# Routed rows turned in 32-blocks by VectorE instead of by TensorE, and loaded in quarters

## The chip, the cores and the metric

The kernel runs on one core of one Trainium2 chip. The core has TensorE (PE, matrix products), VectorE (DVE), ScalarE (ACT), GpSimd (POOL) and SyncE (SP); SP issues most of the loads and stores, POOL issues the indirect ones, and 16 DMA engines carry them. The metric is the device time of one execution in microseconds (us). The kernel before takes 1947.31 us, the median of three runs (1946.74 to 1948.36).

## What is computed

The program is a model of two layers on T = 2048 rows of D = 512 float32 features. Layer 0 is a recurrence over time with a feed-forward part of two experts. Layer 1 is an attention over 16 heads whose older keys are averaged in blocks of 64, and a mixture of experts. Only the second mixture is touched by the change. Cut to what matters it is:

```python
x = x + attn0(norm(x)) * silu(ffn0(norm(x)))      # layer 0
flat = layernorm(x)                               # layer 1: 2048 x 512
h = relu(flat @ shared_w1 + shared_b1)            # two shared experts, 512 -> 352 -> 512
out = flat + h @ shared_w2 + shared_b2            # summed over the two
scores = sigmoid(flat @ centroids.T) + bias       # 16 routed experts
gating = top_4(scores) / sum(top_4(scores))
for w1, b1, w2, b2, g in routed_experts:
    out += (relu(flat @ w1 + b1) @ w2 + b2) * g[:, None]
x = x + attn1(flat) * silu(out)
```

The kernel does not run all 16 experts on all rows: each row goes to its four experts only.

## The kernel before, in words

P = 128 rows make a tile, and NC = 4 chunks of 128 features make a row. The kernel is written in a tile framework. A scheduler at compile time gives each engine a list of instructions from the order of the source, the dependences, and the buffers that each pool has; on the chip each engine runs its list in order and waits on semaphores. A pool's `bufs` says how many tiles of one name may be alive.

**Router stage** (lines 848 to 881, near 990 to 1060 us). In blocks of rows, `xr` is loaded, the first layer's result is added (L854) and statistics are taken (`norm_stats`, L122). L861 writes the normalized row tile into `acc[:, i, 0:D]`, a large array that keeps 544 values (DX) per row: 512 features, 16 gates, the row's number and a flag. `transposed` (L135 to L140) then has PE transpose its four chunks through the PSUM pool `m1y` (two buffers, shared with `pl`), and ACT copies them into `xT`, where features lie on the partitions. After every four tiles, PE forms the 16 expert scores (`pl`, L870). When all are known, the slots are computed, and 64 indirect DMAs of POOL (L1043, names kept in `sent`) write each row of `acc` four times to the DRAM array `xs`, sorted by expert, in tiles of 128 rows. Three further stages lie between: the shared experts (`hidden_shared`, `down_shared`), the fold of attention's weights, and again shared experts. In `down_shared` L1111 adds the normalized rows from `acc` to the result and stores it in `comb`, which starts the sum.

**Routed stage** (lines 1657 to 1741, from 1340 us). The loop over j has 80 tile slots (NRT). Tiles 0 to 64 run always; a slot after them stands in a `tc.If` block, which the count of tiles decides on the chip, and 9 of them ran here, 74 tiles in all. An `If` block is scheduled as a unit of its own: no engine's instruction crosses its edges. One step of the loop does this:

- `hidden_rows(j)`: SP reads the tile's expert number into a register. It issues one DMA for the rows, `x` (L1671, 272 KB, four buffers), which must come after all of `sent`, and four for the weights (`load1`, L654: w1 of 704 KB at L659, w2 of 512 KB at L660, w3 of 192 KB at L661, b2 at L662; three buffers each). The first three tiles load weights ahead of rows, the others after. PE transposes the four chunks (L1678) into `tp`, one PSUM bank of the pool `m1t`. ACT copies `tp` to `xg` (L1680, three buffers). PE forms 12 products (`ph`, L1685: the 352 hidden features in three parts, times 4 chunks; the profile has two instructions for each), and ACT applies bias and relu (`ht`, L942). DVE picks the gate of the tile's expert (`junk`, `g`, L1693) and the row number to write to (`to`, L1698 and L1703).
- a piece of attention for the next tiles (`attend`), which shares PE, DVE, ACT and the PSUM pool `aps` (three banks).
- `down_rows(j - 1)`: three products on PE (`py`, L1709, again two instructions each), the gate multiplied by DVE (`y`, L1714), and two indirect DMAs of POOL that add the two halves of the row to `comb` in DRAM (L1717).

**Last rows** (L1752 to L1769). `comb` is loaded again (L1758), goes through silu on ACT, is multiplied with attention's result (L1765), added to the layer's input (L1768) and stored.

Of the kernel before, what the change touches and what calls it, by code (L numbers as in the profile page):

```python
# [9 lines left out]
F32 = mybir.dt.float32  # L10
I32 = mybir.dt.int32
AF = mybir.ActivationFunctionType
ALU = mybir.AluOpType
AX = mybir.AxisListType
PSUM = bass.MemoryType.PSUM
AFTER = mybir.DependencyInfo(mybir.DependencyClass.Sync, mybir.DependencyReason.DATA)

P = 128
# [49 lines left out]
NF1 = len(FCH)  # L68
NRT = T * KR // P + NR
DX = D + 32  # L70


def bc(ap, axis, shape):
# [4 lines left out]
def tile_kernel(ctx: ExitStack, tc: tile.TileContext, a: dict):  # L78
# [56 lines left out]
    def transposed(pool, src, dst, tag):  # L135

        tp = pool.tile([P, NC, P], F32, tag=tag, name="tp")
        for c in range(NC):
            nc.tensor.transpose(tp[:, c, :], src[:, c * P : (c + 1) * P], ident)
        nc.scalar.copy(dst, tp)  # L140
# [707 lines left out]
    for b in range(NRB):  # L848
# [9 lines left out]
        mv, rstd = norm_stats(xr, n)  # L858
        for s in range(n):
            i = i0 + s  # L860
            nc.vector.tensor_scalar(  # L861
                out=acc[:, i, 0:D], in0=xr[:, s, :], scalar1=mv[:, s, 0:1],
                scalar2=rstd[:, s : s + 1], op0=ALU.subtract, op1=ALU.mult,
            )
            transposed(m1y, acc[:, i, :], xT[:, :, i * P : (i + 1) * P], "py")
        if (i + 1) % (TB // P) == 0:
            t0 = i + 1 - TB // P
            pl = m1y.tile([NR, TB], F32, tag="py", name="pl")
# [230 lines left out]
    def down_shared(tb, hT):  # L1099
        for s in range(TB // P):  # L1100
            t = tb * (TB // P) + s
            py = m1y.tile([P, D], F32, tag="py", name="py")
            for e, w in enumerate(ws):
                for f, n in enumerate(rows_of):
                    nc.tensor.matmul(  # L1105
                        out=py, lhsT=hT[0:n, e, f, s * P : (s + 1) * P],
                        rhs=down(w, f, n), start=(e == 0 and f == 0),
                        stop=(e == NS - 1 and f == NF1 - 1),
                    )
            y = m1s.tile([P, D], F32, tag="y", bufs=3, name="y")  # L1110
            nc.vector.tensor_tensor(out=y, in0=py, in1=acc[:, t, 0:D], op=ALU.add)  # L1111
            for h, c_ in enumerate(comb):
                nc.sync.dma_start(
                    out=c_[t * P : (t + 1) * P, :], in_=y[:, h * D // 2 : (h + 1) * D // 2]
                )
# [200 lines left out]
    logps.close()  # L1316


    aps = ctx.enter_context(tc.tile_pool(name="aps", bufs=3, space=PSUM))
    QB = 256  # L1320

    def softmax(s, heads, keys, neg, wt=None, last=True):
# [206 lines left out]
    sh.close()  # L1529


    m1t = ctx.enter_context(tc.tile_pool(name="m1t", bufs=1, space=PSUM))
    aq = ctx.enter_context(tc.tile_pool(name="aq", bufs=1))
    aq2 = ctx.enter_context(tc.tile_pool(name="aq2", bufs=2))
    fin = ctx.enter_context(tc.tile_pool(name="fin", bufs=NT))
# [121 lines left out]
    def hidden_rows(j):  # L1657
# [9 lines left out]

        if j < FIRST:
            w = weights()
        x = m1x.tile([P, DX], F32, tag="x", bufs=4, name="x")  # L1670
        got = nc.sync.dma_start(out=x, in_=xs[j * P : (j + 1) * P, :])  # L1671
        for name in sent:
            tc.add_manual_dep(got.ins, name, AFTER, reason="any of them may hold its rows")
        if j >= FIRST:
            w = weights()
        tp = m1t.tile([P, NC, P], F32, tag="tp", name="tp")
        for c in range(NC):
            nc.tensor.transpose(tp[:, c, :], x[:, c * P : (c + 1) * P], ident)  # L1678
        xg = m1x.tile([P, NC, P], F32, tag="xg", name="xg")
        nc.scalar.copy(xg, tp)  # L1680
        hT = hts[j % len(hts)]
        for f, n in enumerate(FCH):
            ph = m1ps.tile([P, P], F32, tag="ph", name="ph")
# [7 lines left out]
        junk = m1x.tile([P, NR], F32, tag="junk", name="junk")  # L1691
        g = m1x.tile([P, 1], F32, tag="g", name="g")
        nc.vector.tensor_tensor_reduce(  # L1693
            out=junk, in0=x[:, D : D + NR], in1=oh[:, j, :], scale=1.0, scalar=0.0,
            op0=ALU.mult, op1=ALU.add, accum_out=g,
        )

        nc.vector.scalar_tensor_tensor(  # L1698
            out=junk[:, 0:1], in0=x[:, D + NR + 1 : D + NR + 2], scalar=away[:, 1:2],
            in1=x[:, D + NR : D + NR + 1], op0=ALU.mult, op1=ALU.add,  # L1700
        )
        to = m1x.tile([P, 1], I32, tag="to", bufs=6, name="to")
        nc.vector.tensor_tensor(out=to, in0=junk[:, 0:1], in1=away[:, 0:1], op=ALU.add)  # L1703
# [159 lines left out]
```

## Time and profile before

| What | us | From |
|---|---|---|
| median of three runs | 1947.31 | the times |
| the profiled execution | 1949.3 | the times |
| span of the profiled execution | 1947.6, clock 0.98 | the profile |
| PE, DVE, ACT, POOL busy | 1846.0, 784.7, 527.8, 466.1 | the profile |
| transposes of routed rows (L1678) | 296 instructions, 273 ns each | groups by form |
| copy of the transposed rows (L1680) | 74 instructions, 586 ns each | groups |
| normalizing (L861) | 16 instructions, 548 ns each | groups by form |
| y add of the shared experts (L1111) | 16 instructions, 688 ns each | groups by form |
| DMA over the span | 381.36 MB, 196 GB/s on average | the profile |

Here is how to read a profile of this kind. It is one execution on the chip. A row of a group gives the line, the engine, the operation, output and inputs by name with their shapes, the count, then busy time and the mean of one instruction, then the idle time of the engine just ahead of them and what ended it. PE's matmuls are pipelined, so the mean of one can be longer than the distance to the next. PEld is the load of the stationary operand, which overlaps PE. SPq is SP's issue of a DMA. A table by stage gives busy time and the number of instructions of each engine in a stretch of the span, the granted clock of PE as a share of full speed, and the mean busy share of the 16 DMA engines. The chain of waits follows the work that ended last back to what released it; its rows here are in order of time.

### The profile page before, as it was taken

What the parts mean: (1) busy time and instruction counts of PE and PEld (TensorE: products, weight loads), DVE (VectorE), ACT (ScalarE), POOL (GpSimd) and SP (SyncE); (2) the same over time, 40 slices, a digit from 0 to 9 for tenths busy, and PEclk for the clock granted to TensorE, in tenths of its full rate; (3) what the DMA queues carried; (4) which work ended last, traced back from release to release, by engine and by line L of the source; (5) the groups of instructions that cost most, each with busy time, mean ns of one, the idle gap of its engine ahead of it and who ended that gap; (6) DMA issues with size and microseconds to landing.
All of it is one profiled execution on the core that took longest, in us unless ns stands there. A gap on an engine that the chain in (4) does not pass through costs nothing.

```text
span 1947.6 us, 23278 instructions
## 1 busy us (share of the span) xinstructions
PE 1846.0 (95%) x8107; PEld 1287.3 (66%) x8107; DVE 784.7 (40%) x1581; ACT 527.8 (27%) x997; POOL 466.1 (24%) x350
## 2 busy tenths in 40 slices
PE   5899999999999999999989999999999999999990
PEld 4677777777877777777534744445777777777660
DVE  8713536272725444341276444321332333232213
ACT  6213232232423232321234122221222222222222
POOL 1301112120212010110300561000434443333341
PEclk9899999999999999999999999999999999999995
DMA  7557785625563443437451652025999999888896
GB/s 252 204 172 246 243 288 194 215 94 177 164 224 106 152 141 118 131 126 276 130 182 55 219 191 84 31 81 173 289 311 325 270 279 265 247 250 245 223 273 189
DMA packets 214609, 381.36 MB, mean 196 GB/s; under 512 B 17484, under 2 KB 134988, under 8 KB 213592
## 3 DMA queue, kind: packets, MB, share of 16 engines
q1 hardware_dynamic: 184408, 332.78, 51.3%
q0 software_dynamic: 28784, 45.63, 10.6%
q10 hardware_dynamic: 1296, 1.41, 0.2%
q8 instruction: 67, 1.10, 0.2%
q14 instruction: 54, 0.44, 0.1%
HBM read 294.04 MB, written 85.72 MB: 195 GB/s over the span
## 4 chain that ended last, share of the span: by engine, by line
PE 84%; DMA 6%; DVE 3%; issue 2%; POOL 2%; ACT 2%; SPq 1%; DVEq 0%; POOLq 0%; ACTq 0%
PE pg L571 23%; PE py L593 12%; PE ph L1685 9%; PE py L1709 9%; PE proj L416 7%; PE py L1105 4%; PE ph L956 3%; DMA comb<-y,to 3%; PE pq L1352 2%; PE pw L1593 2%; PE tp L1678 1%; PE ps L1560 1%; PE po L712 1%; PE ps L1566 1%; PE pl L870 1%
## 5 line engine op out<-in xcount | busy, mean ns | idle before, releaser
L571 PE MATMUL pg<-xg,w 128*128 128x256 f32 (+1 forms) x2304 | 495.0, 367 | 3.7 <-ACT xg L563 3.7
L571 PEld LDWEIGHTS pg<-xg,w 128*128 128x128 f32 x2304 | 419.0, 190 | 94.6 <-issue 42.1
L1717 POOL DMA_INDIRECT comb<-y,to x146 | 227.4, 1557 | 343.0 <-DMA comb<-y,to 140.5
L593 PE MATMUL py<-wd,hT 128*128 128x512 f32 x544 | 256.9, 593 | 2.8 <-DVE hT L578 2.8
L1685 PEld LDWEIGHTS ph<-xg,w 128*128 128x128 f32 (+1 forms) x1776 | 202.3, 182 | 37.6 <-ACT xg L1680 31.4
L1685 PE MATMUL ph<-xg,w 128*128 128x128 f32 (+1 forms) x1776 | 213.9, 277 | 1.6 <-DMA w<-in_w_dram 1.6
L1709 PE MATMUL py<-w,ht 128*128 128x512 f32 (+1 forms) x438 | 207.6, 593 | 0.0
L578 DVE TENSOR_TENSOR hT<-sg,pg 128x256 f32<-128x256 f32 (+1 forms) x144 | 56.9, 400 | 335.8 <-ACT sg L576 335.7
L576 ACT ACTIVATE sg<-pg 128x256 f32<-128x256 f32 (+1 forms) x144 | 53.5, 372 | 416.8 <-PE pg L571 416.5
L1714 DVE TENSOR_SCALAR y<-py,g 128x512 f32<-128x512 f32 x73 | 54.6, 748 | 247.6 <-PE py L1709 247.4
L593 PEld LDWEIGHTS py<-wd,hT 128*128 128x128 f32 x544 | 102.1, 190 | 72.1 <-issue 62.0
L942 ACT ACTIVATE ht<-ph,b1t 128x128 f32<-128x128 f32 (+1 forms) x222 | 81.3, 366 | 178.6 <-PE ph L1685 154.2
L1709 PEld LDWEIGHTS py<-w,ht 128*128 128x128 f32 (+1 forms) x438 | 76.7, 191 | 56.2 <-issue 54.0
L1680 ACT COPY xg<-tp 128x512 f32<-128x512 f32 x74 | 43.3, 586 | 179.9 <-PE tp L1678 176.5
L1105 PE MATMUL py<-w,hT 128*128 128x512 f32 (+1 forms) x192 | 89.3, 596 | 0.0
L956 PE MATMUL ph<-xT,w 128*128 128x512 f32 (+1 forms) x192 | 88.0, 597 | 0.0
L1043 POOL DMA_INDIRECT xs<-acc,slot x64 | 63.0, 985 | 67.1 <-DMA xs<-acc,slot 42.8
L712 PE MATMUL po<-wo,yb 128*128 128x512 f32 x128 | 58.4, 612 | 7.6 <-ACT acc L721 3.7
L416 PE MATMUL proj<-xm,wr 128*128 128x256 f32 x256 | 60.5, 391 | 4.3 <-ACT v L452 4.3
L464 POOL TENSOR_TENSOR ex<-st_p,qt 128x1024 f32<-128x1024 f32 x8 | 18.3, 2288 | 193.0 <-DVE qt L463 193.0
L1678 PEld LDWEIGHTS tp<-ident,x 128*128 128x128 f32 x296 | 36.7, 140 | 38.8 <-issue 20.8
L545 POOL DMA_INDIRECT xr<-in_x_dram,tok x17 | 23.2, 1367 | 160.3 <-PE tp L560 133.2
(417 smaller groups left out, 2198.3 us busy)
## 6 DMA issues: line engine op xcount, KB each, us to landing
w<-in_w_dram SPq DMA_DIRECT2D x76, 704.0 KB
w<-in_w_dram SPq DMA_DIRECT2D x76, 512.0 KB
w<-in_w_gate_dram SPq DMA_DIRECT2D x72, 512.0 KB
w<-in_w_up_dram SPq DMA_DIRECT2D x72, 512.0 KB
wd<-in_w_down_dram SPq DMA_DIRECT2D x72, 512.0 KB
xs<-zero SPq DMA_DIRECT2D x16, 1360.0 KB
x<-xs SPq DMA_DIRECT2D x74, 272.0 KB
w<-in_w_dram SPq DMA_DIRECT2D x76, 192.0 KB
```

Source lines behind the costliest of these rows:

```text
L416: nc.tensor.matmul(out=ps[:, j, :], lhsT=w_[:, c, (o0 + j) * P : (o0 + j + 1) * P], rhs=xm[:, c, :], start=(c == 0), stop=(c == NC - 1),)
L571: nc.tensor.matmul(out=pg[:, i, 0:n], lhsT=w[:, c, i * FH + f * P : i * FH + (f + 1) * P], rhs=xg[:, c, 0:n], start=(c == 0), stop=(c == N ...
L578: nc.vector.tensor_tensor(out=hT[:, 0:n], in0=sg[:, 0:n], in1=pg[:, 1, 0:n], op=ALU.mult)
L593: nc.tensor.matmul(out=p, lhsT=hT[:, u * P : (u + 1) * P], rhs=wd[:, f, :], start=first_, stop=last_,)
L712: nc.tensor.matmul(out=po, lhsT=yb[:, c, s * P : (s + 1) * P], rhs=wo[:, c, :], start=(c == 0), stop=(c == NC - 1),)
L942: nc.scalar.activation(dst, src, AF.Relu, bias=b)
L956: nc.tensor.matmul(out=ph[0:n, :], lhsT=up(w, f, n, c), rhs=xT[:, c, cols], start=(c == 0), stop=(c == NC - 1),)
L1043: ins = nc.gpsimd.indirect_dma_start(out=xs, out_offset=bass.IndirectOffsetOnAxis(ap=slot[:, i, k : k + 1], axis=0), in_=acc[:, i, :], in_ ...
L1105: nc.tensor.matmul(out=py, lhsT=hT[0:n, e, f, s * P : (s + 1) * P], rhs=down(w, f, n), start=(e == 0 and f == 0), stop=(e == NS - 1 and f ...
L1685: nc.tensor.matmul(out=ph[0:n, :], lhsT=up(w, f, n, c), rhs=xg[:, c, :], start=(c == 0), stop=(c == NC - 1),)
L1709: nc.tensor.matmul(out=py, lhsT=hT[0:n, f, :], rhs=down(w, f, n), start=(f == 0), stop=(f == NF1 - 1),)
L1717: nc.gpsimd.indirect_dma_start(out=c_, out_offset=bass.IndirectOffsetOnAxis(ap=to, axis=0), in_=y[:, h * D // 2 : (h + 1) * D // 2], in_of ...
```

## The change

It consists of these parts.

- The rows lie in `acc` and `xs` with their 32-feature blocks in another order: feature block q of chunk c, formerly at place 4c + q, lies at place 4q + c. L861 therefore writes the normalized row to a new tile `xn` (two buffers). PE transposes from `xn`, and a new ACT copy puts `xn` into `acc` with its blocks reordered. L1111 reads `acc` with a matching access pattern.
- The load of a routed tile is split: for each q of 4, one DMA takes 128 columns of the tile's 128 rows (64 KB) and puts them onto 32 partitions, so that partition 32q + r holds row r of each 32-row block. A fifth DMA loads the last 32 columns into `own`, with a row to a partition. All five depend on `sent`.
- One DVE instruction, `nc.vector.transpose`, turns the 32x32 blocks of `x` and writes `xg`. PE's four transposes and ACT's copy are gone.
- `junk` and `to` take their inputs from `own` instead of from `x`.
- The PSUM pool `m1t` goes, and `aps` gets a fourth bank.

```diff
--- before.py
+++ after.py
@@ -68,6 +68,8 @@
 NF1 = len(FCH)
 NRT = T * KR // P + NR
 DX = D + 32
+NB = 4
+BL = P // NB
 
 
 def bc(ap, axis, shape):
@@ -858,11 +860,17 @@
         mv, rstd = norm_stats(xr, n)
         for s in range(n):
             i = i0 + s
+            xn = tr.tile([P, D], F32, tag="xn", bufs=2, name="xn")
             nc.vector.tensor_scalar(
-                out=acc[:, i, 0:D], in0=xr[:, s, :], scalar1=mv[:, s, 0:1],
+                out=xn, in0=xr[:, s, :], scalar1=mv[:, s, 0:1],
                 scalar2=rstd[:, s : s + 1], op0=ALU.subtract, op1=ALU.mult,
             )
-            transposed(m1y, acc[:, i, :], xT[:, :, i * P : (i + 1) * P], "py")
+            transposed(m1y, xn, xT[:, :, i * P : (i + 1) * P], "py")
+
+            nc.scalar.copy(
+                acc[:, i, 0:D].rearrange("p (q c k) -> p q c k", q=NB, k=BL),
+                xn.rearrange("p (c q k) -> p q c k", q=NB, k=BL),
+            )
         if (i + 1) % (TB // P) == 0:
             t0 = i + 1 - TB // P
             pl = m1y.tile([NR, TB], F32, tag="py", name="pl")
@@ -1108,7 +1116,11 @@
                         stop=(e == NS - 1 and f == NF1 - 1),
                     )
             y = m1s.tile([P, D], F32, tag="y", bufs=3, name="y")
-            nc.vector.tensor_tensor(out=y, in0=py, in1=acc[:, t, 0:D], op=ALU.add)
+            nc.vector.tensor_tensor(
+                out=y.rearrange("p (c q k) -> p c q k", q=NB, k=BL),
+                in0=py.rearrange("p (c q k) -> p c q k", q=NB, k=BL),
+                in1=acc[:, t, 0:D].rearrange("p (q c k) -> p c q k", q=NB, k=BL), op=ALU.add,
+            )
             for h, c_ in enumerate(comb):
                 nc.sync.dma_start(
                     out=c_[t * P : (t + 1) * P, :], in_=y[:, h * D // 2 : (h + 1) * D // 2]
@@ -1316,7 +1328,7 @@
     logps.close()
 
 
-    aps = ctx.enter_context(tc.tile_pool(name="aps", bufs=3, space=PSUM))
+    aps = ctx.enter_context(tc.tile_pool(name="aps", bufs=4, space=PSUM))
     QB = 256
 
     def softmax(s, heads, keys, neg, wt=None, last=True):
@@ -1529,7 +1541,6 @@
     sh.close()
 
 
-    m1t = ctx.enter_context(tc.tile_pool(name="m1t", bufs=1, space=PSUM))
     aq = ctx.enter_context(tc.tile_pool(name="aq", bufs=1))
     aq2 = ctx.enter_context(tc.tile_pool(name="aq2", bufs=2))
     fin = ctx.enter_context(tc.tile_pool(name="fin", bufs=NT))
@@ -1667,17 +1678,25 @@
 
         if j < FIRST:
             w = weights()
-        x = m1x.tile([P, DX], F32, tag="x", bufs=4, name="x")
-        got = nc.sync.dma_start(out=x, in_=xs[j * P : (j + 1) * P, :])
-        for name in sent:
-            tc.add_manual_dep(got.ins, name, AFTER, reason="any of them may hold its rows")
+
+        x = m1x.tile([P, NB, NC, BL], F32, tag="x", bufs=4, name="x")
+        own = m1x.tile([P, DX - D], F32, tag="own", bufs=4, name="own")
+        mine = xs[j * P : (j + 1) * P, :]
+        loads = [
+            nc.sync.dma_start(
+                out=x[q * BL : (q + 1) * BL].rearrange("p b c k -> p b (c k)"),
+                in_=mine[:, q * P : (q + 1) * P].rearrange("(b r) k -> r b k", r=BL),
+            )
+            for q in range(NB)
+        ]
+        loads.append(nc.sync.dma_start(out=own, in_=mine[:, D:]))
+        for got in loads:
+            for name in sent:
+                tc.add_manual_dep(got.ins, name, AFTER, reason="any of them may hold its rows")
         if j >= FIRST:
             w = weights()
-        tp = m1t.tile([P, NC, P], F32, tag="tp", name="tp")
-        for c in range(NC):
-            nc.tensor.transpose(tp[:, c, :], x[:, c * P : (c + 1) * P], ident)
         xg = m1x.tile([P, NC, P], F32, tag="xg", name="xg")
-        nc.scalar.copy(xg, tp)
+        nc.vector.transpose(xg.rearrange("p c (b r) -> p b c r", r=BL), x)
         hT = hts[j % len(hts)]
         for f, n in enumerate(FCH):
             ph = m1ps.tile([P, P], F32, tag="ph", name="ph")
@@ -1691,13 +1710,13 @@
         junk = m1x.tile([P, NR], F32, tag="junk", name="junk")
         g = m1x.tile([P, 1], F32, tag="g", name="g")
         nc.vector.tensor_tensor_reduce(
-            out=junk, in0=x[:, D : D + NR], in1=oh[:, j, :], scale=1.0, scalar=0.0,
+            out=junk, in0=own[:, 0:NR], in1=oh[:, j, :], scale=1.0, scalar=0.0,
             op0=ALU.mult, op1=ALU.add, accum_out=g,
         )
 
         nc.vector.scalar_tensor_tensor(
-            out=junk[:, 0:1], in0=x[:, D + NR + 1 : D + NR + 2], scalar=away[:, 1:2],
-            in1=x[:, D + NR : D + NR + 1], op0=ALU.mult, op1=ALU.add,
+            out=junk[:, 0:1], in0=own[:, NR + 1 : NR + 2], scalar=away[:, 1:2],
+            in1=own[:, NR : NR + 1], op0=ALU.mult, op1=ALU.add,
         )
         to = m1x.tile([P, 1], I32, tag="to", bufs=6, name="to")
         nc.vector.tensor_tensor(out=to, in0=junk[:, 0:1], in1=away[:, 0:1], op=ALU.add)
```

## The prediction

> **What bounds the kernel.** I read the page first, then a table of busy time by stage, then the groups of instructions by form, the timeline of the last tiles, and the waits.
>
> ```profile
> PE 1846.0 (95%) x8107; PEld 1287.3 (66%) x8107; DVE 784.7 (40%) x1581; ACT 527.8 (27%) x997; POOL 466.1 (24%) x350
> ```
>
> TensorE is busy for 95% of the span. The change acts in the router stage (1013 to 1060 us) and in the routed stage (from 1340 on), so those rows decide. Columns: us, then busy time and count of PE, PEld, DVE, ACT, POOL, then clock, DMA share, GB/s.
>
> ```profile
> 1013.00:1043.00 30.00, 25.42 (x114) 10.77 (x112) 14.77 (x32) 12.96 (x25) 0.00 (x0) 1.00 0.05 18
> 1043.00:1060.00 17.00, 17.00 (x44) 7.49 (x45) 13.67 (x54) 7.37 (x13) 2.06 (x8) 1.00 0.35 110
> 1340.00:1348.00 8.00, 6.23 (x34) 4.69 (x32) 3.11 (x16) 1.76 (x3) 0.39 (x2) 1.00 0.90 304
> 1348.00:1839.00 491.00, 490.81 (x2708) 355.16 (x2708) 145.19 (x462) 125.83 (x296) 193.24 (x124) 1.00 0.94 272
> 1839.00:1898.00 59.00, 57.10 (x335) 40.44 (x334) 11.81 (x46) 16.36 (x40) 24.85 (x16) 1.00 0.95 280
> 1898.00:1948.00 50.00, 0.00 (x0) 0.00 (x0) 19.35 (x32) 11.14 (x17) 9.31 (x6) 0.50 0.64 185
> ```
>
> From 1348 to 1839 us PE is busy for 490.8 of 491 us at full clock, with tiles 0 to 63: 7.67 us a tile, attention pieces included. DMA runs at 0.94 beside it, so it is second, and not far off. After 1898 PE has nothing to do: the scatter-adds and the last rows finish.
>
> What the four transposes really take of PE, the timeline of one tile in the `If` blocks shows (start, us, engine, line):
>
> ```profile
> 1856.98 0.60 PE L1678 MATMUL tp<-ident,x 128*128 128x128 f32 x4
> ...
> 1857.41 1.02 PE L1709 MATMUL py<-w,ht 97*128 97x512 f32 x2
> ...
> 1858.31 2.92 PE L1685 MATMUL ph<-xg,w 128*128 128x128 f32 x24
> ```
>
> The next instruction starts 0.43 us after the first transpose, and the chain of waits lists each set as 0.44 us of path. The page's 273 ns for one of them is latency; four of those would be 1.09 us, far too much. The 24 matmuls follow xg without a hole.
>
> **The saving.** PE loses 4 transposes a tile: 0.435 us, 7.67 becomes 7.24 in the middle. The sets of tiles 0 to 2 lie in PE's wait for the first weights (1342.8 to 1348.2; the row `PE ph L1685 <- DMA w<-in_w_dram` ends it) and save nothing. Tiles 3 to 64: 62 × 0.435 = **27.0 us**. The last 9 tiles are in the tail below. ACT loses 74 copies of 586 ns, off the path.
>
> **The transpose on DVE.** No DVE transpose is in this trace. Rows near it, 128x512 f32 on DVE: 548 ns (L861), 688 (L1111), 748 (L1714). The Trainium skill ("VectorE: DVE Perf Modes", section "The three transpose paths") speaks against the move: it sends a 128×128 transpose to TensorE and gives VectorE 311 ns for one of bf16, so four would be 1.24 us, an estimate. By the row I take 0.65; ends 0.55 and 1.24. Either way 74 of them are 41 to 92 us on an engine that is busy for 145 of 491 us, so the middle stage hides it. The condition is that it runs ahead: the scheduler puts the small gate operation `junk`, which depends on the same load, as early as its three buffers let it, and xg has three buffers too. In an `If` block it can't cross the block's edge: it stands behind y of the tile before (0.75 us), and PE may wait up to 0.2 + 0.75 + 0.65 + 0.15 = 1.75 us a tile. This goes into the tail.
>
> **The loads.** One DMA of x (272 KB, 128 packets of 2176 B at 88 ns in the records = 0.70 us of 16 engines) becomes four of 64 KB and one of 16 KB. The records show 27 ns for packets of 512 B: 512 × 27 + 128 × 10 (small ones, estimated) = 15.1 us / 16 = 0.95, so +0.25 us of DMA a tile. The skill ("SBUF — State Buffer", section "Door 1: The DMA port swizzle") says that 32 neighbouring partitions reach only 8 of 16 ports, 27.2 GB/s each: 64 KB then take 0.30 us, four 1.2, about +0.6 by estimate. The trace's nearest case, sixteen loads of `vo` onto 16 partitions each, shows 84 ns for packets of 2048 B, as on 128 partitions. I take +0.25; ends 0.2 and 0.6. Against some 5.9 us of demand a tile, 6.2 to 6.5 still fit in 7.24.
>
> The queue is the worse matter. SP issues in order, 0.47 us apart:
>
> ```profile
> 1506.85 0.37 SPq L659 DMA_DIRECT2D w<-in_w_dram  x1
> 1507.32 0.37 SPq L1671 DMA_DIRECT2D x<-xs  x1
> 1507.78 0.40 SPq L1344 DMA_DIRECT2D sn<-in_sin_dram  x1
> ```
>
> Five DMAs for one are +4 × 0.47 = 1.9 us of SP a tile, hidden while SP waits:
>
> ```profile
> SPq L660 <- PE py L1709: 221.9, 57, 7.0
> ...
> SPq L660 <- DMA w<-in_w_dram: 8.5, 6, 2.4
> ```
>
> 222 us over 57 tiles is 3.9 us of slack a tile, less 0.43 for the shorter period: 1.5 stay. But SP's DMAs share eight completion semaphores: in the `vo` loads seven leave by 1290.4, the eighth only at 1294.4, when the first has landed. Each DMA waits for the eighth before it. Today a tile has 5 DMAs, so 1.6 tiles are in flight; then 9, and 0.9 of a tile: w1 of a tile can leave only after that of the tile before has landed, about 1.0 us earlier. The period is at least 1.0 + landing time of w1. That is 5.85 us in the middle (9 in 10 under 6.8): 6.85 against 7.24, so PE still decides, with 0.4 to spare. I add 1 us for tiles where it doesn't. Queued behind a waiting load on SP are the weights of its tile, cs, sn and xo; PE waits for the weights.
>
> **Start and early tiles.** Fifteen loads instead of three stand ahead of what follows, 12 × 0.47 = 5.6 us if all are in front; three of them were issued ahead of the weights of 1342.3. Part can go in the hole before. Ends 0 and 5, I take **+3**. In the first ten tiles weights arrive 1 to 2 us ahead of PE, landing in up to 9.8 us: ten savings of 0.435 are lost to them, **+4**.
>
> **Router stage.** The normalized row goes to `xn`, with two buffers, so normalizing, formerly done ahead (990 to 1013) for most rows, must wait for PE's transposes and ACT's new copy. ACT gains 16 copies; SBUF-to-SBUF copies of 512 elements take 548 to 720 ns here, I take 0.63: 10 us beside 13 of 30. DVE gains about 13 us beside 14.8 of 30. Neither fills the stage, but each pl group of four tiles (3.6 us of PE) now waits for DVE, PE, ACT in turn, two buffers deep: four groups by about 1 us, **+4**, ends 0 and 10. The block order in the y add (16 × 688 ns, in 203 us where PE is full) costs nothing; should it double, 11 us stay hidden there. The fourth bank for attention's scores can only take waits away from 1060 to 1137, where PE idles 2.75 of 77: **−1**, ends −3 and 0.
>
> **Tail.** In the last 9 tiles the path is already the scatter-adds', about 6.9 us a tile from 1854 to 1917, PE's 5.8 under it:
>
> ```profile
> 1854.47 6.34 DMA comb<-y,to
> ...
> 1861.54 5.96 DMA comb<-y,to
> ...
> 1868.33 6.07 DMA comb<-y,to
> ```
>
> The blocks reuse the same semaphores in the same order, 9 loads for 8, so b2 waits for the first x load of its own block, and the next block's first load for b2: 9 × 0.5 + 4.4 (landing of b2 there) ≈ 8.9 us a tile. SP enters two tiles ahead (15 us), so PE ends 9 × 8.9 − 15 − 59 = 6 us later relative to its start, while the backlog of scatter-adds (20 us after PE now) shrinks. **+3**, ends −8 and +12.
>
> **Sum.** −27.0 + 4 (early) + 3 (start) + 4 (router) − 1 (bank) + 3 (tail) + 1 (queue) = −13 on the profiled 1949.3 (span 1947.6 and 1.7 around it): 1936. The profiled execution is 2.0 above the median of 1947.3, so **1934 us**, −0.7%. A measurement of this kernel can tell 0.2%, 3.9 us: faster is below 1943.4, slower above 1951.2.
>
> **Rivals.**
> A, slower: the eight semaphores bound the routed stage. The weights of the next tile no longer load beside this tile's, so every tile takes 1.0 + landing time. It cancels the saving from a landing of 6.7 us on (1.0 + 6.7 = 7.67), against 5.85 now and 6.8 in the slow tenth; the five loads add traffic that lengthens it. At 6.9 the period is 7.9: 62 × 0.23 = +14, with start, router and tail +10: 1971. Against it: fewer loads in flight land sooner, and DMA has room. 0.28, mostly 1953 to 1975.
> B, nothing: the middle saves its 27, but router (+10), start (+5), early tiles (+4) and tail (+8) at their upper ends give it all back: 1947. 0.14.
> C, all of it: the losses hide in existing waits and the tail gains with PE, −27 − 2: 1918 to 1920. 0.11.
> D, it doesn't do what it says: DVE's transpose stands behind y, as in the `If` blocks, in every tile, and PE waits 1.75 for 0.435 saved: 64 × 1.3 = +84, 2030. The early `junk` speaks against it: 0.03.
> The forecast has 0.44, from 1924 to 1944.
>
> Range: leaving out D, the far part of A and half of C: 1917 to 1966. Faster 0.54 (0.43 of the forecast, C), same 0.14 (B and an edge), slower 0.32 (A, D, a rest of B).
>
> **What would show it.** The middle stage's PE time per tile should be 7.2 us with PE still full and no tp rows; a hole at `PE ph <- DMA w` or SP's waits for `DMA w` or `DMA x` growing by 60 us or more shows A; `PE ph <- DVE xg` shows D. DVE's transpose row should read 550 to 1240 ns. SP's x loads in the last blocks should come some 9 us apart. The router stage should be 31 to 40 us long instead of 30, and the first ph start 3 us later after pq. The largest doubt is w1's landing time at 9 loads a tile: half a microsecond turns the sign.

## The result, and the profile after

The changed kernel takes 1975.36 us (median of four runs, 1974.10 to 1982.43) against 1947.84 us for the kernel before on the same occasions (1946.74 to 1951.71). The ratio is 1.0133, with a 95% interval of 1.0113 to 1.0152: slower, where 1934 us and a gain of 0.7% had been forecast, and outside the range of 1917 to 1966 us. The profiled execution of the changed kernel took 1982.4 us, with a span of 1980.7 us. It is the longest of the four runs, so its sums are some 7 us above the median.

PE's share of the span fell from 95 to 92%, in the page's first part:

```profile
PE 1826.9 (92%) x7811; PEld 1268.4 (64%) x7811; DVE 818.6 (41%) x1655; ACT 493.2 (25%) x941; POOL 468.0 (24%) x350
```

The stages come next, in the table by stage (us, then busy time and count of PE, PEld, DVE, ACT, POOL, then clock, DMA share, GB/s). The rows are the router stage, the hole ahead of the first ph, tiles 0 to 63, the last tiles, and the last rows.

```profile
1018.00:1057.00 39.00, 29.96 (x113) 11.52 (x112) 28.87 (x66) 25.60 (x47) 0.00 (x0) 0.87 0.30 108
1351.00:1365.00 14.00, 12.55 (x52) 9.41 (x50) 5.68 (x13) 0.00 (x0) 1.11 (x6) 1.00 0.72 235
1365.00:1874.00 509.00, 468.24 (x2445) 333.74 (x2445) 173.92 (x532) 89.32 (x234) 196.00 (x126) 0.99 0.97 262
1874.00:1940.00 66.00, 52.36 (x294) 36.08 (x294) 16.71 (x56) 10.96 (x30) 28.80 (x19) 1.00 0.94 247
1940.00:1981.00 41.00, 0.00 (x0) 0.00 (x0) 19.36 (x32) 11.24 (x17) 2.25 (x2) 0.52 0.66 213
```

The reader is to see two things. PE did lose the work: from 490.8 to 468.2 us for the same 64 tiles. But the stage grew from 491 to 509 us, since PE now stands still in it. The view of waits (engine, line, releaser, then us in total, times, longest), for the stretch from 1340 to 1945 us, says where. These are all of PE's rows in it:

```profile
PE ph L1704 <- DVE xg L1699: 39.4, 28, 1.5
PE ps L1577 <- DVE qg L1377: 7.4, 4, 2.2
PE pw L1604 <- ACT sT L1601: 7.1, 11, 0.7
PE ph L1704 <- issue: 1.5, 1, 1.5
```

In the kernel before, PE's two rows there come to 2.0 us, and the longer of them is the first weights:

```profile
PE ph L1685 <- DMA w<-in_w_dram: 1.6, 1, 1.6
```

In the changed kernel no row names a load: neither x nor w. PE waits for VectorE's turn of its own tile; the row with `issue` is the first tile's. Of the 28 waits for xg, 9 are in the `If` blocks and 19 in tiles 1 to 64. The timeline of one tile shows the pattern (start, us, engine, line, and in brackets the idle time before it and its releaser):

```profile
1897.56 2.74 PE L1728 MATMUL py<-w,ht 128*128 128x512 f32 x6
...
1900.34 0.75 DVE L1733 TENSOR_SCALAR y<-py,g 128x512 f32<-128x512 f32 x1 [5.08 <-PE py L1728]
1901.01 0.70 DVE L1699 STREAM_TRANSPOSE xg<-x 128x512 f32<-128x512 f32 x1
...
1901.76 2.92 PE L1704 MATMUL ph<-xg,w 128*128 128x128 f32 x24 [1.46 <-DVE xg L1699]
```

VectorE's list has the turn of the next tile behind y, and y waits for py. PE's list has that tile's ph right behind py. So y (0.75 us) and the turn (0.70 us) run while PE has nothing to do, 1.46 us. In the kernel before, the last third of py stood between the transposes and ph and hid ACT's copy. PE's list changed as well. Before, ph of a tile, pieces of attention and py of an earlier tile alternate, and py stands right behind its own ph in 2 of the first 65 tiles; now it does so in all 65. Attention's pieces stand together between the tiles, where PE has the second and third row of waits.

The loads were not late. Counted from their semaphores, the five row loads of tile 70 leave SP from 1899.7 us on and have landed at 1905.7; its turn starts at 1914.9. In the middle it is the same: those of tile 30 have landed at 1588.0, its w1 at 1589.6, and its ph starts at 1603.5.

SP's own waits (from 1330 to 1950 us) did change, and would mislead if read alone. L661 is the issue of w1, L662 that of w2:

```profile
SPq L661 <- DMA w<-in_w_dram: 53.3, 49, 2.6
...
SPq L662 <- PE py L1728: 24.6, 26, 1.1
```

SP now waits for landed loads, where it waited 222 us for a weight buffer that py had to free. With the first row it runs into its eight semaphores; but as PE waits for no load, this is time that SP had to spare.

The 33 us between the two profiles, stage by stage (by the ends of the last `po`, the last `pl`, the first ph, the last product of PE and the last row):

| Stretch | before | after | difference |
|---|---|---|---|
| up to the last `po` (not touched by the change) | 1013.5 | 1018.2 | +4.8 |
| router stage, to the last `pl` | 29.5 | 38.7 | +9.2 |
| to the first ph of a routed tile | 305.2 | 308.0 | +2.8 |
| to PE's last product | 547.9 | 574.6 | +26.7 |
| to the end | 51.5 | 41.2 | −10.3 |

The fourth row is PE's busy time 547.9 to 520.7 (−27.2) and its holes 0 to 53.9.

In the router stage the chain of waits shows two of the four groups of scores in the kernel before (start, us, what):

```profile
1024.64 3.62 PE pl L870 x8
1031.97 3.62 PE pl L870 x8
```

and the second and third of them in the changed kernel, with loads of ACT's function table around the third (L133 is the square root of the statistics, L798 the sigmoid of the scores):

```profile
1029.72 5.32 PE pl L878 x8
...
1036.23 1.28 ACT L798
...
1040.25 1.28 ACT L133
...
1042.37 6.16 PE pl L878 x8
```

The eight products of a group are the same work; their granted clock was 1.00 before, and 0.68 and 0.59 in these two.

### The profile page after: what moved, and what is told of

Its sections match the earlier page's. It is cut to its first block, busy times and chain, and to the rows that moved or that the text cites. A ratio compares the mean times of both kernels' runs of the same rounds, so it can differ in the third digit from the quotient of the medians.

```text
span 1980.7 us, 23066 instructions
## 1 busy us (share of the span) xinstructions
PE 1826.9 (92%) x7811; PEld 1268.4 (64%) x7811; DVE 818.6 (41%) x1655; ACT 493.2 (25%) x941; POOL 468.0 (24%) x350
## 3 DMA queue, kind: packets, MB, share of 16 engines
q0 software_dynamic: 28784, 45.63, 10.3%
## 4 chain that ended last, share of the span: by engine, by line
PE 77%; DMA 10%; issue 3%; DVE 3%; ACT 2%; POOL 2%; SPq 1%; DVEq 0%; ACTq 0%; POOLq 0%
PE pg L573 23%; PE py L595 11%; PE ph L1704 8%; PE proj L418 7%; PE py L1728 7%; PE py L1113 4%; PE ph L964 3%; DMA w<-in_w_dram 3%; DMA comb<-y,to 3%; PE pq L1364 2%; PE pw L1604 2%; PE po L714 1%; PE ps L1571 1%; PE pl L878 1%; DVE xg L1699 1%
## 5 line engine op out<-in xcount | busy, mean ns | idle before, releaser
L1704 PEld LDWEIGHTS ph<-xg,w 128*128 128x128 f32 (+1 forms) x1776 | 207.2, 185 | 74.5 <-DVE xg L1699 62.6
L1704 PE MATMUL ph<-xg,w 128*128 128x128 f32 (+1 forms) x1776 | 216.0, 279 | 40.9 <-DVE xg L1699 39.4
L1728 PE MATMUL py<-w,ht 128*128 128x512 f32 (+1 forms) x438 | 200.2, 593 | 0.0
L578 ACT ACTIVATE sg<-pg 128x256 f32<-128x256 f32 (+1 forms) x144 | 53.4, 371 | 419.6 <-PE pg L573 419.3
L418 PEld LDWEIGHTS proj<-xm,wr 128*128 128x128 f32 x256 | 49.4, 194 | 16.5 <-ACT v L454 5.8
L418 PE MATMUL proj<-xm,wk 128*128 128x256 f32 x256 | 59.7, 388 | 0.0
```

The lines of the kernel that those rows point to most:

```text
L418: nc.tensor.matmul(out=ps[:, j, :], lhsT=w_[:, c, (o0 + j) * P : (o0 + j + 1) * P], rhs=xm[:, c, :], start=(c == 0), stop=(c == NC - 1),)
L1704: nc.tensor.matmul(out=ph[0:n, :], lhsT=up(w, f, n, c), rhs=xg[:, c, :], start=(c == 0), stop=(c == NC - 1),)
L1728: nc.tensor.matmul(out=py, lhsT=hT[0:n, f, :], rhs=down(w, f, n), start=(f == 0), stop=(f == NF1 - 1),)
```

## The experiments

Each ratio is to the kernel before on the same chip, with its 95% interval. "Holes" are PE's idle time between the first ph and its last product, from the profile of the run. "Close" is the number of the first 65 tiles whose py stands right behind its own ph in PE's list; it is 2 in the kernel before and 65 in the changed one.

**One load (e1).** The four quarter loads and `own` become the one load of the kernel before; the turn stays on VectorE.

```diff
-        loads = [nc.sync.dma_start(out=x[q * BL : (q + 1) * BL]..., in_=mine[:, q * P : (q + 1) * P]...) ...]
-        loads.append(nc.sync.dma_start(out=own, in_=mine[:, D:]))
+        got = nc.sync.dma_start(out=x, in_=xs[j * P : (j + 1) * P, :])
```

> The changed kernel with x loaded again by one DMA of 272 KB, a row to a partition; VectorE turns the 32x32 blocks of that tile, and the gate reads its last columns from it. The rows are then not where the products want them, so only the time is meant. Theory 'order' (nine loads a tile instead of five make the scheduler write py of a tile right behind its ph, and the turn of tile k+1 right behind y of tile k, so PE waits 1.46 us where no attention piece lies between): with five loads the turns stand two tiles ahead and py one tile late, the waits of ph for xg in tiles 0 to 64 fall from 28 us to under 5, the waits in attention's pieces (14 us) go too, tiles 0 to 64 take some 465 us instead of 509, the router stage keeps its 9 us: about 1937 us. Rival 'turn' (the turn on VectorE holds PE up whatever the loads are): the 1.46 us holes stay, 1965 to 1975. Rival 'semaphores' (loads land too late with nine a tile) gives 1937 as well and is not told apart here.

Measured: 1936.32 us, ratio 0.9916 (0.9890 to 0.9942). From the first ph to PE's last product 518.9 us instead of 574.6, holes 6 us, and no wait for xg among them; the waits inside attention's pieces are gone too. Close is 3. In VectorE's list the turn of a tile mostly stands behind y of the tile five before it; in the changed kernel it stands behind y of the tile just before it. So the turn itself, 701 ns on VectorE, does not hold PE; how the loads are written does, directly or through the lists. The number was expected (some 1937), but a rival, loads that land too late, gives the same.

**The five loads with PE's transposes (e2).**

```diff
-        nc.vector.transpose(xg.rearrange("p c (b r) -> p b c r", r=BL), x)
+        tp = m1t.tile([P, NC, P], F32, tag="tp", name="tp")
+        for c in range(NC):
+            nc.tensor.transpose(tp[:, c, :], x[:, c].rearrange("p c k -> p (c k)"), ident)
+        nc.scalar.copy(xg, tp)
```

> The changed kernel with its five row loads, but with the four transposes on PE and the copy on ACT as before (and three banks for attention again); the rows are not where the products want them, so only the time is meant. Theory 'order': the loads land some ten us ahead of their tile, so PE never waits for a load; the transposes of the next tile can be placed ahead of py, so no 1.46 us holes; what stays is up to 14 us of waits in attention's pieces and 9 us of the router stage: 1955 to 1968 us. Rival 'semaphores': the routed stage stays as slow as in the changed kernel or slower by the 27 us of transposes, 1975 to 2000, and SP's waits for landed loads stay near 110 us.

Measured: 1988.16 us, ratio 1.0190 (1.0172 to 1.0208). By the number alone this is the rival's. Its waits for the same stretch are not:

```profile
PE ph L1708 <- ACT xg L1703: 26.3, 36, 0.7
PE pw L1605 <- ACT sT L1602: 4.9, 11, 0.8
```

PE waits for loads for 0.7 us in all. The lists changed here too: in 36 tiles the transposes stand right ahead of ph, and ACT's copy (0.7 us) lies open. My number for the "order" theory was wrong because I took it that the transposes would stay ahead of py.

**The turn one tile ahead (e3).** The load and turn of tile j+1 are written in step j. Number, size and queue of the loads stay.

```diff
+        if j == 0:
+            turned.append(turned_rows(0))
+        if j + 1 < NRT:
+            turned.append(turned_rows(j + 1))
...
+        xg, own = turned.pop(0)
```

> The changed kernel with the five row loads and the turn of tile j+1 written in step j, ahead of the products of tile j, in the If blocks too. Everything else, the number of loads too, is as in the changed kernel. Theory 'order': the 29 holes of 1.46 us ahead of ph go, in tiles 0 to 64 (28 us) and in the If blocks (13 us, of which the scatter-adds behind give back about half); the waits in attention's pieces stay: 1938 to 1948 us. Rivals 'semaphores' and 'turn': no change, 1970 to 1978.

Measured: 1958.81 us, ratio 1.0031 (1.0019 to 1.0042), about 20 us less than the changed kernel's ratio gives on this chip, but not quite the forecast. Tiles 0 to 63 take 482.5 us instead of 509.0, and the whole stretch 548.4 instead of 574.6. This is the cleanest test. Close is 65 as in the changed kernel, and the turn stands one y further ahead. The row loads are issued a tile earlier too, but they had lain ready before. The 28 waits for xg are gone. All waits of PE over 5 us that are left:

```profile
PE ph L1713 <- DMA w<-in_w_dram: 11.7, 6, 3.2
PE ps L1577 <- DVE qg L1377: 7.2, 4, 2.2
PE pw L1604 <- ACT sT L1601: 7.1, 11, 0.7
```

The first row is new: with PE faster, the weights become the next limit, above all in the `If` blocks (w1 of tile 66 lands at 1855.1, its ph starts at 1855.3). That is a wait for loads, as rival A has it, at some 7 us a tile, behind the one that decided. Whether the eight semaphores hold the loads back or the DMA engines, which are busy throughout there (share 1.02 from 1841 to 1907 us), these rows don't tell.

**The router part alone, on the kernel before (e4).**

```diff
+            xn = tr.tile([P, D], F32, tag="xn", bufs=2, name="xn")
             nc.vector.tensor_scalar(
-                out=acc[:, i, 0:D], in0=xr[:, s, :], scalar1=mv[:, s, 0:1],
+                out=xn, in0=xr[:, s, :], scalar1=mv[:, s, 0:1],
...
+            nc.scalar.copy(acc[:, i, 0:D], xn)
```

> The kernel before with one part of the change alone: the normalized row goes to xn (two buffers), PE transposes from xn, and ACT copies it to acc in the old block order. Theory: the statistics of later rows slip behind the scores of earlier ones, ACT changes its table six times where it did once, and the router stage is 8 to 10 us longer with nothing after it to take that up: 1955 to 1958 us. Rival (the stages behind it take it up, and the 9 us seen between the profiles is their own spread): 1946 to 1950.

Measured: 1963.11 us, ratio 1.0055 (1.0034 to 1.0075): +11 us, a little over the 8 to 10 expected, with 39.5 us from the last `po` to the last `pl`, and 548.8 us with PE full in the routed stage. So the router part costs its 9 to 11 us by itself.

**The quarter loads on ACT's queue (e5).**

```diff
-            nc.sync.dma_start(
+            nc.scalar.dma_start(
                 out=x[q * BL : (q + 1) * BL].rearrange("p b c k -> p b (c k)"),
```

> The changed kernel with the four quarter loads of x issued by ACT's queue instead of SP's; own and the weights stay on SP. Nine DMAs a tile, their bytes and their packets are as in the changed kernel. Theory 'order' (in a form the first runs allow: what turns the order of PE's and VectorE's lists is how many loads stand in SP's queue a tile, and the chip's DMA is not the limit): py comes one tile late, the turns two tiles ahead, tiles 0 to 64 take 457 to 470 us instead of 509, the total is as with one load, 0.990 to 0.995 of the kernel before. Rival 'packets' (the stage is slow because 512 B packets onto 32 partitions and nine DMAs load the DMA engines): tiles 0 to 64 stay at 500 to 510, 1.010 to 1.014 of the kernel before.

Measured: 2001.61 us, ratio 1.0252 (1.0216 to 1.0287). In the number neither theory. The lists, though, are the good ones, as the first theory had it: close is 3, and the turn stands behind y of the tile five before it, as with one load, although the loads themselves, their 32 partitions and their count are those of the changed kernel. But the loads now stand in ACT's list, and what is queued behind them there is relu:

```profile
ACT ht L950 <- DMA x<-xs: 101.7, 23, 7.7
```

ACT stands still for 102 us in front of relu until an x load has landed. PE's holes are 58 us; its longest rows are 26.5 us for xg, whose rows now come late, and 18.2 for `ht`. The run says nothing on packets; it shows what a load costs on an engine that also computes.

**No router part (e6), and both together (e7, e8).** The rows stay in their natural order, and the routed w1 is laid out in the turned order as an input.

```diff
-    o["w1"] = both("w1").reshape(NE, NC, P, F1).transpose(0, 2, 1, 3)
+    w1 = both("w1")
+    turned = w1[:NR].reshape(NR, NB, NC, BL, F1).transpose(0, 2, 1, 3, 4)
+    w1 = np.concatenate([turned.reshape(NR, D, F1), w1[NR:]], axis=0)
+    o["w1"] = w1.reshape(NE, NC, P, F1).transpose(0, 2, 1, 3)
```

> The changed kernel without its router part: the rows keep their natural block order in acc and in DRAM, as in the kernel before, and the rows of the routed experts' w1 are laid out in the turned order instead, by the host's layout of the input. Loads, turn and all the rest as in the changed kernel. Theory: the router stage is back to its old length, 10 us less than in the changed kernel, and nothing else moves: 1.007 to 1.009 of the kernel before. Rival (the routed stage moves with it, since the order of the lists is drawn up anew): outside 1.005 to 1.011.

> Both together: w1 laid out in the turned order, the rows natural, the quarter loads of x on ACT's queue. If the two losses are separate they add up: 0.985 to 0.990 of the kernel before, some 1924 us. If one of them only hid the other, 0.990 to 0.995 as with the queue alone.

> As the run before, and the turn of tile j+1 written in step j, so that it stands ahead of y in the If blocks too. Theory: the holes of 1.46 us in the last nine tiles go (13 us of PE); the scatter-adds, some 6.9 us a tile there, take back half or more: 0.981 to 0.988. Rival (the tail is the scatter-adds' alone): the same as the run before within 0.2%.

Measured: e6 1968.31 us, 1.0088 (1.0053 to 1.0123), as expected: the router stage is back at 31.2 us (29.5 before; the 1.7 left is one group of scores at the lower clock, 5.3 us), and the routed stage has the same holes, 53.9 us. e7 1985.91 us, 1.0161 (1.0124 to 1.0197), and e8 1973.49 us, 1.0110 (1.0080 to 1.0141): ACT's stall is in both, so these two miss for the reason of e5.

**The turn ahead, natural rows, fewer loads (e9, e10, e11).** e9 joins e3 and e6. e10 also lays w2, w3 and b2 out as one block, so that a tile has seven loads. e11 also holds py behind the next ph.

```diff
-        nc.sync.dma_start(out=w2, in_=pick(a["w2"])[:, 0 : NF1 - 1, :])
-        nc.sync.dma_start(out=w3[0:last, :], in_=pick(a["w2"])[0:last, NF1 - 1, :])
-        nc.sync.dma_start(out=w3[last : last + 1, :], in_=row(a["b2"]))
+        nc.sync.dma_start(out=w2, in_=pick(a["w2"]))
```

> The turn written one tile ahead and the natural rows (w1 laid out in the turned order) together; nine loads a tile, all on SP. If the two gains are separate: 1.0031 less 0.0045 = 0.9986 of the kernel before (0.997 to 1.000). PE's waits for w of some 13 us, mostly in the If blocks, stay, since the nine loads are still there.

> As the run before, with w2, w3 and b2 of an expert laid out in one block and loaded by one DMA of 768 KB: seven loads a tile instead of nine, 62 KB more a tile. Theory: with the turn out of the way the eight semaphores are the next limit (w1 of a tile leaves when a load of the tile before has landed), in the If blocks first; with seven loads PE's waits for w fall from 13 us to under 4, and the total to 0.992 to 0.996 of the kernel before. Rival (the waits for w are DMA bandwidth): the larger load lengthens them, 0.999 or more.

> As the run before, and in tiles 0 to 64 py of a tile is held behind ph of the next tile on PE, as in the kernel before. Theory: with the turn ahead it no longer matters whether py follows its ph at once; what waits inside attention's pieces (14 us) depends on where those lie, and stays: the same as the run before within 0.2%. Rival (the adjacent ph and py cost by themselves, through the relu between them): 5 to 12 us less.

Measured: e9 1952.23 us, 0.9995 (0.9980 to 1.0009); e10 1952.47 us, 0.9993 (0.9981 to 1.0006); e11 1955.16 us, 1.0012 (1.0001 to 1.0024). e9 is as expected; e10 misses its 0.992 to 0.996, and by the number it is the rival's. PE's waits of ph for w fell from 14.0 us in e9 to 1.6 in e10, but 10.8 us of waits for xg came in their place. Those lie in the `If` blocks and come from the scatter-adds: y waits for one of an earlier tile (8.0 us for `DMA comb<-y,to` ahead of 1848.0 us), the turn stands behind y, and PE's next ph starts after a hole of 2.8 us at 1849.4. The last scatter-adds and rows took 54.3 us instead of 46.1 after PE's end. e11 has the same seven loads and waits 9.1 us for w again. So that the number of loads is what holds w back isn't shown; the scatter-adds would stand behind it in any case. e11 is level with e10 to within 0.2%, as expected: once the turn is ahead, py next to its ph costs nothing that can be told.

**Column quarters (e12).** Four loads of x as before in number, bytes and packets, but of 128 rows on 128 partitions each.

```diff
-                out=x[q * BL : (q + 1) * BL].rearrange("p b c k -> p b (c k)"),
-                in_=mine[:, q * P : (q + 1) * P].rearrange("(b r) k -> r b k", r=BL),
+                out=x[:, q].rearrange("p c k -> p (c k)"),
+                in_=mine[:, q * P : (q + 1) * P],
```

> The changed kernel with its four x loads taken as four column quarters of 128 rows, on 128 partitions instead of 32 each; 64 KB, 128 bytes a block as before, packets of 512 B, five row loads, the turn on VectorE. The rows are not where the products want them, so only the time is meant. If the 32 partitions cost the DMA engines time, packets of 512 B last shorter here than the median of 27 ns and mean of 36 ns of the changed kernel, and the loads of x land sooner than its 4.9 us; theory: neither changes by over 10%. In this kernel's lists the turns stand one y further ahead in most tiles, so the holes ahead of ph go outside the If blocks: 1.002 to 1.007 of the kernel before; if ports or packets were the cause, 1.013 or, with ports relieved, under 1.000.

Measured: 1944.89 us, ratio 0.9953 (0.9937 to 0.9968), 1.8% below the changed kernel. The forecast for these lists (1.002 to 1.007) missed, and a ratio under 1.000 was the sign named for ports. The records speak against ports all the same. Packets of 512 B have a median of 27 ns here as there (mean 33 and 36), and the loads of x land 5.0 us after their issue here and 4.9 there. So the 32 partitions cost no DMA time that these runs show. What differs are the lists: the turn is one y further ahead in 42 of the first 65 tiles (close is 64), and PE's waits for xg are 9.5 us (9 times) instead of 39.4. PE's holes are 21 us instead of 54, which is the gain.

**Row blocks (e13 to e16).** The four loads are cut by 32-row blocks, each spread over the four groups of partitions, with every value at the place that the changed kernel gives it.

```diff
-                out=x[q * BL : (q + 1) * BL].rearrange("p b c k -> p b (c k)"),
-                in_=mine[:, q * P : (q + 1) * P].rearrange("(b r) k -> r b k", r=BL),
+                out=x[:, b].rearrange("p c k -> p (c k)"),
+                in_=mine[b * BL : (b + 1) * BL, 0:D].rearrange("r (q k) -> q r k", q=NB),
```

> The changed kernel with its four x loads cut by 32-row blocks instead of by quarters: each of the four takes all 512 columns of 32 rows and spreads its four quarters over the four groups of 32 partitions, so that it lands on 128 partitions. Bytes, packets, count and the place of every value in x are those of the changed kernel, nothing else is touched. Its lists of VectorE and PE are those of the run with column quarters. Theory: it does as that run, 0.993 to 0.997 of the kernel before; the cut of the loads alone is then worth 35 us, through the lists. If the misplaced rows had a part in that run's gain: 1.005 or more.

> The run before with the natural rows (w1 laid out in the turned order, no xn and no copy). If the gains add up: 0.995 less 0.0045, 0.988 to 0.993 of the kernel before, some 1930 us.

> The run before with the turn written one tile ahead. Theory: the holes ahead of ph in the If blocks go (9 of 1.46 us), but there the eight semaphores with nine loads hold w back, as in the earlier run with the turn ahead: within 0.3% of the run before.

> The run before with w2, w3 and b2 in one load, seven loads a tile. Theory: PE's waits for w in the If blocks go, PE's holes from the first ph to the last py fall under 15 us, 0.984 to 0.990 of the kernel before. Rival (the scatter-adds and the last loads decide the end whatever PE does): as the run before.

Measured: e13 2044.46 us, 1.0457 (1.0417 to 1.0497); e14 2030.69, 1.0396; e15 2035.43, 1.0419; e16 2020.15, 1.0335. All four miss by far, and the records point to one reason, which lies in the cut: the outermost dimension of such a load's source is 4. The records show the packets of 512 B with six or more under way during 9 of 400 us (from 1400 us on), against 72 in the changed kernel, at the same 27 ns a packet; in e13 exactly four are under way for 60 us, longer than any other number. The loads of x land 6.7 us after their issue instead of 4.9, and PE waits for weights, which stand behind them on SP:

```profile
PE ph L1704 <- DMA w<-in_w_dram: 65.4, 34, 4.1
```

The Trainium skill ("DMA: Bandwidth & Descriptors", section "Rules for kernel authors") says that a transfer whose outermost dimension has fewer than 16 elements is confined to at most that many DMA engines. The count of packets under way agrees. It also means that e13 does not confirm e12: the same lists of VectorE and PE, another transfer.

**Eight buffers for xn (e17).** `bufs=2` becomes `bufs=8`.

> The changed kernel with eight buffers for xn instead of two. Theory: two buffers hold the statistics back behind PE's transposes, and with eight they run ahead again, ACT changes its table less often, and of the router stage's extra 10 us some 6 go: 1.009 to 1.011 of the kernel before. Rival (the 10 us are ACT's 16 new copies themselves): 1.012 to 1.014, as the changed kernel.

Measured: 1977.48 us, 1.0127 (1.0108 to 1.0145). In its profile the stretch from the last `po` to the last `pl` is 33.9 us instead of 38.7, so about half of the stage's loss goes with more buffers (ACT loads its table three times instead of five; two groups of scores still run at the lower clock, 5.2 and 5.3 us). The time, however, is the rival's: the run isn't told from the changed kernel, and from PE's last product to the end 44.4 us passed instead of 41.2. How much of the 9 us the buffers cost in the whole stays open.

**One load, natural rows, turn ahead (e18).** The edits of e1, e6 and e3 together.

> The floor of the idea: x in one load of 272 KB, a row to a partition (so the rows are not where the products want them, and only the time is meant), natural rows with w1 laid out in the turned order, the turn on VectorE written one tile ahead. Theory: the run with one load was at 0.9916; without the router's 9 us and the If blocks' holes of 13 us, half of which the scatter-adds give back: 0.981 to 0.986 of the kernel before. Rival (the scatter-adds pace the end whatever PE does): 0.986 to 0.990.

Measured: 1925.45 us, 0.9871 (0.9842 to 0.9900). By the number that is the rival's. PE's holes are 5 us, its stretch 519.0 us; but from PE's last product to the end it is 53.4 us, where the scatter-adds and the last rows finish. This is what the move of the transposes would be worth if nothing had to be paid for the layout. It is no version that can be used, since its rows lie wrong; of the kernels whose rows lie right, none was found that is faster than the kernel before.

## Why the prediction was wrong

- **The saving held.** PE's busy time over the routed stage fell by 27.2 us. It was to be 27.0 for tiles 3 to 64; over all 74 tiles it is 32.2, less some 5 us for a granted clock of 0.99 instead of 1.00 in that profile.
- **The turn's price held.** It takes 701 ns, where 0.65 was taken between 0.55 and 1.24. The 1.24 us, estimated from the Trainium skill's price of one bf16 transpose ("VectorE: DVE Perf Modes", "The three transpose paths"), is 1.8 times the measured one. The loss is not the turn's own: with one load it stands on VectorE too, and the kernel is faster (e1, 0.9916).
- **The step that failed** is the condition under it: "The condition is that it runs ahead". I read from `junk`, which the scheduler had put early, that the turn would be put early too. `junk` was early in a list that was drawn up for one load a tile. With the quarter loads the scheduler drew up other lists for PE and VectorE: the turn stood behind y in the middle stage too, and PE waited for it 28 times, 39.4 us in all, mostly 1.46 us at a time. e3 moves the turn ahead of that y: these waits go, and the stretch is 26 us shorter. The forecast had this hole, up to 1.75 us, for the 9 tiles in `If` blocks (measured 1.46) and, as rival D, for every tile at 0.03; it came in 19 tiles of the other 65 too. A case between "never" and "always" was not counted.
- **The waits inside attention's pieces**, 14.5 us, were not in the forecast at all. They go with PE's list: they are gone in e1, where pieces, ph and py alternate again, and stay in e3, where they don't.
- **Rival A came near in its number (1971) and was wrong in its mechanism.** The eight semaphores are there: SP waits 53 us for loads of w at L661. But w1 lands in 4.2 us instead of 5.85 (medians of tiles in the middle), which makes A's period 5.2 us where it was to be 6.85. That fewer loads in flight land sooner, as was said against A, holds for w1 alone: w2 takes 6.0 us instead of 4.8, and w3 5.75 instead of 4.65. Even so, w1 had landed 13 us ahead of its ph (median; the least is 5 us). SP's loads in the last blocks came 7 us apart, not 9. The sign that I had named for A, a growth of SP's waits for loads by 60 us, was there (25 us before, 110 after, over the weights and the row loads), and it was a bad sign: SP's waits cost only when PE waits for SP.
- **The router stage** was given +4, ends 0 and 10, and cost 9.2 (e4: 11 in the time). The term was mis-sized. Two things were missing in it. One is ACT's changes of table: statistics (a square root) and scores (a sigmoid) alternate once the rows can't run ahead, which makes five table loads of 1.28 us from 1026 to 1051 us, where the kernel before had one, at 1021; four of the five lie on the chain of waits. The other is the granted clock: two groups of scores took 5.3 and 6.2 us instead of 3.6, together 4.2 us. In every run with this router part two or three of the four groups ran so, in the runs without it none or one. What lowers the clock there is not shown.
- **Start** was +3 and is +2.8; **the bank** was −1, and no run shows it apart. **The tail** was +3, ends −8 and +12: 10.3 us came back after PE's end, where fewer scatter-adds are left when PE comes later; the `If` blocks' own holes, 13 us, stand among the holes below.
- In the sum: the saving −27 for −27, holes +54 where 4 were counted (early tiles, queue and bank), router +9 for +4, start +3 for +3, tail −10 for +3: +28 (from the unrounded figures) in place of −13. The rest of the 33 us, 4.8, lies ahead of everything that the change touches; the medians differ by 27.5.

What stays open is why the scheduler draws up these lists. For PE's list the runs narrow it down. Close is 2 or 3 in all runs with five loads a tile on SP, e5, e7 and e8 among them, where the four quarters go to the same 32 partitions but stand on ACT's queue. With seven or nine loads on SP it is 50 to 65, except in e11, where the source holds py back. So PE's list goes with the number of loads on SP's queue, not with their partitions or with their number over all queues. The place of the turn in VectorE's list moves with the pattern of the loads too (e12, with nine). The traces show the lists, not the scheduler's reasons.

## What to carry to other kernels

Where a compile-time scheduler orders the engines' lists, an edit of the loads, even of the queue that issues them, can reorder products that it doesn't touch. So for an instruction moved to another engine, count not only whether that engine has room, but what stands directly ahead of it in its list and whether PE's next product is queued behind that; write it a tile ahead in the source if it matters. And a queue that waits often is no bound until the engine that sets the end waits for what it brings: read PE's own rows of waits first.

## What the runs showed of the hardware

- A DVE transpose of 128x512 f32 in 32x32 blocks took 701 ns (median of 74, 700 to 712).
- Packets of 512 B onto 32 partitions lasted as long as onto 128 (median 27 ns both, mean 36 and 33), and the loads landed in 4.9 and 5.0 us. The Trainium skill's rule on ports ("SBUF — State Buffer", "Door 1: The DMA port swizzle": 32 neighbouring partitions reach 8 of 16 ports), from which +0.6 us a tile had been estimated as the upper end, has no counterpart in these records, at least beside the other loads that were under way.
- Loads of x whose outermost dimension is 4 landed in 6.7 us instead of 5.0 with the same bytes, packets and lists of VectorE and PE: 1.0457 against 0.9953 (e13, e12).
- Eight products of one group of scores took 3.6 us at a granted clock of 1.00, 5.3 at 0.68 and 6.2 at 0.59.
- Loads put on ACT's queue stopped ACT in front of its relu for 102 us (e5).
